# The opening of a triangle-and-pair kernel: weights turned ahead of x, evacuated on ScalarE, and the output weights prepared twelve steps later

## Chip, cores and metric

The kernel runs on one core of a Trainium2 chip. The metric is the device time of one execution in microseconds (us); the time before is the median of 3 runs, 3340.28 us (3338.49 to 3342.46).

## What is computed

x has the shape 1 x 384 x 384 x 128. Layer 0 is a triangle multiplication; layer 1 is a gated pair layer on its result. All in float32.

```python
z_n = layernorm(z, norm_g, norm_b)
a = linear(z_n, Wa, ba) * sigmoid(linear(z_n, Wga, bga))
b = linear(z_n, Wb, bb) * sigmoid(linear(z_n, Wgb, bgb))
x = einsum('bijd,bjkd->bikd', a, b)
x = layernorm(x, normo_g, normo_b)
z = z + linear(x, Wo, bo) * sigmoid(linear(z_n, Wgo, bgo))        # layer 0
left, right = z @ W_left + b_left + (z @ W_eq + b_eq), z @ W_right + b_right
out = left * right.sum(axis=2, keepdims=True) * sigmoid(z @ W_gate + b_gate)
y = layernorm(out @ W_out + b_out + z, ln_scale, ln_bias)          # layer 1
```

The change touches only the first projections (Wa, Wga, Wb, Wgb, Wgo with their biases) and the preparation of Wo and of layer 1's constants.

## The kernel before

The work has three stages: the projections of x (to about 1.4 ms), one 384 x 384 x 384 product per channel, and the output of layer 0 with all of layer 1. The order of every engine's instructions is the order of the Python text: there is no scheduler, each engine has its own queue and works it off in order, and a tile's buffer is given out again when its last reader is done. The change lies in the first stage.

x is read in tiles of 16 columns (fetch, fetch_parts), 128 rows each; the first tile comes in four parts of four columns. A step (step(s)) treats four columns, so a tile has four steps and the stage 288. For each four columns VectorE takes the statistics (L141, L142), POOL makes the factors rstd and off (norm_factors, L148 to L151), ScalarE normalises (normalise, zn, L160), TensorE turns the result (turn, ptr, L180) and ScalarE copies it out of PSUM (turned_out, zT, L191). Step s then projects zT on ga, a, gb and b (L246: pga, pa, pgb, pb) and on go (gate_project, pgo, L211). ScalarE does the sigmoids sga and sgb (L251) and gt (L198); VectorE combines pa with sga into at (L263), pb with sgb into bt (L276), and adds gate_bias to pgo (gs, L213). Step s also turns step s+1's columns. All projections share six PSUM buffers (pool p1p, tag pk), the turned x has two (tag ptr). From step 12 (CATCH_UP) on, POOL also adds b_out to each next tile of x and stores it as Z (residual, L171, L172), in the second step of a tile; before that four tiles are done at fixed steps.

The normalisation's gain and shift are folded into the weights: prepare(k) (L297) turns a weight on TensorE, copies it to SBUF as raw (L302), scales it by norm_g into wT (L304), multiplies raw by norm_b on TensorE (L306 for go, L309) and adds that to the bias (L310, or L307 for gate_bias, which is the row r_bgo broadcast to all partitions). The weights are loaded through ACT's queue (L339), everything else through SP's. Before the first step the text alternates quarters of x with weights: quarter 0; prepare ga, a; turn and evacuate quarter 0; quarter 1; prepare gb, b; quarter 2; nb_w (a broadcast of norm_b, L375); prepare go; quarter 3 (L364 to L377).

last_weights (L313 to L333) prepares Wo and layer 1's constants in three pieces, one after each of the steps 12, 13 and 14 (L381). The first piece is the copy of ob_w (L315), center, the turn of Wo (pt_o, which takes one of the six PSUM buffers) and two evacuations (raw_o, scaled_o); the third multiplies them (both_o, L327, L328).

## Time and profile before

| | |
|---|---|
| median of 3 runs | 3340.28 us |
| the profiled execution's own time | 3343.24 us |
| its span, first to last instruction | 3341.5 us |
| TensorE busy | 3293.7 us, 99% of the span |
| VectorE, ScalarE, POOL busy | 2666.1, 2311.3, 2091.9 us |
| mean granted TensorE clock | 0.994 |
| step 0's first projection (pga) starts | 15.00 us |
| one step in the steady part of the stage | 4.77 us |

The profile is one execution. Times in the views count from the first instruction of the span. A row of the timeline gives start, length, engine, line, operation, what is written from what, and, in brackets, how long the engine had been idle and what ended the wait. The engines are PE (TensorE), PEld (its weight loads, which overlap PE), DVE (VectorE), ACT (ScalarE), POOL and SP; a q behind a name is the queue that issues. The chain of work follows back, from the end, what released each piece. The clock column of the windows shows no throttle in the first 19 us even where the matmuls' lengths do, since its record begins later.

### The profile page before, as it was taken

How to read it: one execution, taken by the hardware profiler on the slowest of the kernel's cores; microseconds unless marked ns; L12 is line 12 of the kernel's file. 1: busy time of each engine (PE TensorE's matmuls, PEld its weight loads, DVE VectorE, ACT ScalarE, POOL GpSimd, SP SyncE). 2: the span in 40 equal slices, each digit the busy share in tenths (PEclk: the TensorE clock that was granted, in tenths of full speed). 3: DMA queues.
4: the chain of work that ended last, by engine and by line, in shares of the span. 5: the costliest groups of instructions: out<-in, count | busy, mean ns of one | idle time of the engine just before them, and what ended most of it. 6: DMA issues, size and time to landing. Idle time of an engine off the chain costs nothing.

```text
span 3341.5 us, 53397 instructions
## 1 busy us (share of the span) xinstructions
PE 3293.7 (99%) x15581; PEld 2191.3 (66%) x15581; DVE 2666.1 (80%) x8599; ACT 2311.3 (69%) x5488; POOL 2091.9 (63%) x1574
## 2 busy tenths in 40 slices
PE   8999999999999999999999999999999999999997
PEld 5555555555555555555555555588888888888885
DVE  8877777777777777455555555799999999999998
ACT  7778787877777788522222222378888888888887
POOL 7555555555555555355555555358888888888887
PEclk9999999999999999999999999999999999999998
DMA  6889899889888889899999999767777777777774
GB/s 226 265 256 273 278 282 282 278 279 281 280 269 264 268 275 282 254 337 318 312 315 311 312 311 304 258 231 262 261 263 262 262 262 264 264 263 263 263 265 142
DMA packets 675522, 910.52 MB, mean 272 GB/s; under 512 B 319520, under 2 KB 616480, under 8 KB 647712
## 3 DMA queue, kind: packets, MB, share of 16 engines
q1 hardware_dynamic: 634192, 680.28, 63.9%
q0 software_dynamic: 40320, 226.51, 19.3%
q8 instruction: 126, 2.06, 0.2%
q14 instruction: 164, 1.34, 0.1%
q10 hardware_dynamic: 720, 0.33, 0.0%
HBM read 454.04 MB, written 452.98 MB: 271 GB/s over the span
## 4 chain that ended last, share of the span: by engine, by line
PE 96%; DVE 2%; POOL 1%; DMA 1%; ACT 0%; issue 0%; POOLq 0%; ACTq 0%; SPq 0%; DVEq 0%
PE pm L488 22%; PE pga L246 8%; PE pa L246 7%; PE pgb L246 7%; PE pb L246 7%; PE py L602 7%; PE pf L592 7%; PE pgo L211 7%; PE pleft L643 7%; PE pg L645 7%; PE ptr L180 4%; PE ptr L566 4%; DMA G<-gt 0%; DVE py L608 0%; PE pg L656 0%
## 5 line engine op out<-in xcount | busy, mean ns | idle before, releaser
L488 PE MATMUL pm<-ab 128*128 128x384 f32 x2304 | 746.6, 487 | 5.8 <-DVE gs L213 5.8
L488 PEld LDWEIGHTS pm<-ab 128*128 128x128 f32 x2304 | 438.9, 191 | 312.4 <-DVE gs L213 6.7
L507 POOL TENSOR_TENSOR acc<-acc,xd 128x384 f32<-128x384 f32 x381 | 380.1, 998 | 362.4 <-DVE xd L500 362.2
L505 ACT ACTIVATE sq<-xd 128x384 f32<-128x384 f32 x381 | 188.5, 495 | 542.3 <-DVE xd L500 542.2
L276 DVE SCALAR_TENSOR_TENSOR bt<-pb,c_L_conv_bb,sgb 128x512 f32<-128x512 f32 x288 | 320.9, 1114 | 243.3 <-ACT zT L191 218.6
L160 ACT ACTIVATE zn<-xt,off,rstd 128x128 f32<-128x128 f32 x1152 | 503.3, 489 | 2.9 <-POOL off L151 2.8
L635 ACT ACTIVATE res<-res,off,rs 128x128 f32<-128x128 f32 x1152 | 482.5, 486 | 18.4 <-POOL off L629 15.7
L500 DVE TENSOR_TENSOR xd<-pm,acc 128x384 f32<-128x384 f32 x381 | 212.2, 557 | 343.3 <-POOL acc L507 321.3
L608 DVE SCALAR_TENSOR_TENSOR py<-py,acc,gr 128x128 f32<-128x128 f32 x1152 | 433.7, 377 | 2.2 <-PE py L602 1.6
L267 POOL DMA_DIRECT2D A<-at x72 | 85.4, 1186 | 539.2 <-DVE at L263 539.2
L251 ACT ACTIVATE sga<-pga,c_L_conv_bga 128x512 f32<-128x512 f32 x288 | 197.9, 687 | 267.6 <-PE pga L246 267.6
L211 PEld LDWEIGHTS pgo<-wT_go,zT 128*128 128x128 f32 x2176 | 285.7, 192 | 130.0 <-issue 66.5
L613 DVE BATCH_NORM_STATS2 st<-res 128x6 f32<-128x128 f32 x1152 | 361.4, 315 | 0.3
L675 POOL TENSOR_TENSOR res<-res,r_L_conv_ln_bias 128x1536 f32<-128x1536 f32 x94 | 324.6, 3453 | 7.4
L171 POOL TENSOR_TENSOR acc<-xt,r_L_conv_b_out 128x2048 f32<-128x2048 f32 x72 | 327.4, 4548 | 1.8
L592 PE MATMUL pf<-w_o,h 128*128 128x128 f32 x2304 | 321.2, 276 | 6.1 <-ACT w_o L574 5.3
L674 POOL TENSOR_TENSOR res<-res,r_L_conv_ln_scale 128x1536 f32<-128x1536 f32 x94 | 325.3, 3461 | 0.2 <-issue 0.2
L650 ACT ACTIVATE sg<-pg,c_L_conv_b_gate 128x384 f32<-128x384 f32 x384 | 223.0, 581 | 144.5 <-PE pg L645 92.6
L602 PE MATMUL py<-w_o,xr 128*128 128x128 f32 x2304 | 321.1, 276 | 0.0
L643 PE MATMUL pleft<-pairT,m_L_conv_W_left 128*128 128x384 f32 x768 | 313.1, 489 | 2.8 <-ACT pairT L568 2.8
L645 PE MATMUL pg<-pairT,m_L_conv_W_gate 128*128 128x384 f32 x768 | 311.1, 487 | 0.0
L141 DVE BATCH_NORM_STATS2 st<-xt 128x6 f32<-128x128 f32 x1152 | 305.5, 265 | 3.7 <-DMA xt<-in_x_dram 3.6
(142 smaller groups left out, 6826.8 us busy)
## 6 DMA issues: line engine op xcount, KB each, us to landing
A<-at POOLq DMA_DIRECT2D x72, 1024.0 KB, 8.5
Z<-acc POOLq DMA_DIRECT2D x72, 1024.0 KB, 8.2
G<-gt POOLq DMA_DIRECT2D x72, 1024.0 KB, 9.2
xr<-X SPq DMA_DIRECT2D x96, 768.0 KB, 6.0
gr<-G SPq DMA_DIRECT2D x96, 768.0 KB, 7.6
zr<-Z SPq DMA_DIRECT2D x96, 768.0 KB, 8.8
X<-xd SPq DMA_DIRECT2D x381, 192.0 KB, 6.2
xt<-in_x_dram SPq DMA_DIRECT2D x71, 1024.0 KB, 17.9
```

The lines of the kernel that those rows point to most:

```text
L160: nc.scalar.activation(g["zn"][:, c, :], g["x"][:, c, :], AF.Identity, bias=g["off"][:, c : c + 1], scale=g["rstd"][:, c : c + 1],)
L211: nc.tensor.matmul(pgo[:, c, :], lhsT=zT[:, c, :], rhs=wT["go"], start=True, stop=True)
L246: nc.tensor.matmul(pk, lhsT=wT[k], rhs=zT, start=True, stop=True)
L488: nc.tensor.matmul(products[d, ib], lhsT=ab[:, 0, q, ib * P : (ib + 1) * P], rhs=ab[:, 1, q, :], start=(q == 0), stop=(q == NB - 1),)
L507: nc.gpsimd.tensor_tensor(s1[:, ib, :], s1[:, ib, :], xd, ALU.add)
L592: nc.tensor.matmul(pf[:, q, :], lhsT=h[:, q * P : (q + 1) * P], rhs=w_o, start=True, stop=True)
L602: nc.tensor.matmul(py[:, q, :], lhsT=g["x"][:, i, q * P : (q + 1) * P], rhs=w_o0, start=True, stop=True)
L608: nc.vector.scalar_tensor_tensor(py[:, q, :], py[:, q, :], rs0[:, q, u : u + 1], g["g"][:, i, q, :], ALU.mult, ALU.mult)
L613: nc.vector.bn_stats(b["st"][:, k, q, :], b["res"][:, k, q, :])
L635: nc.scalar.activation(g["res"][:, i, q, :], g["res"][:, i, q, :], AF.Identity, bias=g["off"][:, i, q : q + 1], scale=g["rs"][:, i, q : q ...
L643: nc.tensor.matmul(pleft, lhsT=w_left, rhs=pairT, start=True, stop=True)
L645: nc.tensor.matmul(pg[:, 0:N], lhsT=w_gate, rhs=pairT, start=True, stop=True)
```

## The change

The five weights' turns are put ahead of x on TensorE, behind ten turns of the identity; two more such turns stand between the bias matmuls and x's first quarter (keep_busy). The copies out of PSUM and the scalings of all five weights go from VectorE to ScalarE, and so do the four bias columns; gate_bias's addition stays on VectorE and comes after all four quarters' statistics. Quarter 1's statistics move ahead of the normalisation of quarter 0. The loads of gb, b and go go through POOL's queue. Two of the parts of x are issued earlier among SP's small loads. The raw copies have five buffers instead of two. last_weights begins after step 24.

```diff
-        def prepare(k):
+        def turn_weight(k):
             both = ppp.tile([P, CT, P], FP, tag="pk", name="w_" + k)
-            pt, pb = both[:, 0, :], both[:, 1, :]
-            nc.tensor.transpose(pt, wT[k], ident)
-            raw = wp.tile([P, P], FP, tag="raw", name="raw_" + k, bufs=2)
-            nc.vector.tensor_copy(raw, pt)
-            scaled = ctile([P, P], "wT_" + k)
-            nc.vector.tensor_scalar(scaled, raw, ng, None, ALU.mult)
-            if k == "go":
-                nc.tensor.matmul(pb, lhsT=nb_w, rhs=raw, start=True, stop=True)
-                nc.vector.tensor_tensor(gate_bias, pb, gate_bias, ALU.add)
-            else:
-                nc.tensor.matmul(pb[:, 0:1], lhsT=raw, rhs=nb, start=True, stop=True)
-                nc.vector.tensor_tensor(bcol[k], pb[:, 0:1], bcol[k], ALU.add)
-            wT[k] = scaled
+            nc.tensor.transpose(both[:, 0, :], wT[k], ident)
+            return both
+
+        def raw_weight(k):
+            raw = wp.tile([P, P], FP, tag="raw", name="raw_" + k, bufs=5)
+            nc.scalar.copy(raw, halves[k][:, 0, :])
+            return raw
+
+        def scale_weight(k):
+            wT[k] = ctile([P, P], "wT_" + k)
+            nc.scalar.activation(wT[k], raws[k], AF.Copy, scale=ng)
...
-        for k in ("ga", "a", "gb", "b", "go"):
+        for k in ("ga", "a"):
             weight(k, nc.scalar)
+        for k in ("gb", "b", "go"):
+            weight(k, nc.gpsimd)
         nc.scalar.activation(warm, mhalf, AF.Sigmoid)
         ng, nb = column(L0 + "norm_g"), column(L0 + "norm_b")
         for k in ("ga", "a", "gb", "b"):
+            if k in ("ga", "gb"):
+                next(x_parts)
             bcol[k] = column(L0 + "b" + k)
-            if k in ("a", "b"):
-                next(x_parts)
...
+        def keep_busy(times):
+
+            idle = ppt.tile([P, CT, P], FP, tag="ptr", name="idle")
+            for k in range(times):
+                nc.tensor.transpose(idle[:, k % CT, :], ident, ident)
+
+        halves, raws = {}, {}
+        gated_and_not = ("ga", "a", "gb", "b")
+        keep_busy(10)
         first_quarter(0)
+        nc.vector.tensor_copy(nb_w, nb.to_broadcast([P, P]))
+        for k in gated_and_not + ("go",):
+            halves[k] = turn_weight(k)
+        for k in gated_and_not:
+            raws[k] = raw_weight(k)
+            scale_weight(k)
+        for k in gated_and_not:
+            nc.tensor.matmul(halves[k][:, 1, 0:1], lhsT=raws[k], rhs=nb, start=True, stop=True)
+        first_quarter(1)
         normalise(0, 0)
-        prepare("ga")
-        prepare("a")
+        keep_busy(2)
         turn(0)
+        raws["go"] = raw_weight("go")
         turned_out(0)
-        first_quarter(1)
+        for k in gated_and_not:
+            nc.scalar.activation(bcol[k], halves[k][:, 1, 0:1], AF.Identity, bias=bcol[k])
+        scale_weight("go")
+        pb = halves["go"][:, 1, :]
+        nc.tensor.matmul(pb, lhsT=nb_w, rhs=raws["go"], start=True, stop=True)
         normalise(0, 1)
-        prepare("gb")
-        prepare("b")
         first_quarter(2)
-        nc.vector.tensor_copy(nb_w, nb.to_broadcast([P, P]))
-        prepare("go")
         first_quarter(3)
+        nc.vector.tensor_tensor(gate_bias, pb, gate_bias, ALU.add)
         later = last_weights()
         for s in range(NT * TS):
             step(s)
-            if s >= CATCH_UP:
+            if s >= 2 * CATCH_UP:
                 next(later, None)
```

More of the change, by code (lines that the diff above doesn't have):

```diff
@@ L318, in last_weights @@
             nc.tensor.transpose(pt, wT["o"], ident)
-            raw, scaled = (wp.tile([P, P], FP, tag="raw", name=k + "_o", bufs=2) for k in ("raw", "scaled"))
+            raw, scaled = (wp.tile([P, P], FP, tag="raw", name=k + "_o", bufs=5) for k in ("raw", "scaled"))
             nc.vector.tensor_copy(raw, pt)
```

## The prediction

> **What bounds the kernel now.** I read the page first, then the chain of work for the first 30 us, then the timeline of the opening and of the place where the output weights are prepared. The page's busy times, and under them the chain that ended last, by engine:

> ```profile
> PE 3293.7 (99%) x15581; PEld 2191.3 (66%) x15581; DVE 2666.1 (80%) x8599; ACT 2311.3 (69%) x5488; POOL 2091.9 (63%) x1574
> ...
> PE 96%; DVE 2%; POOL 1%; DMA 1%; ACT 0%; issue 0%; POOLq 0%; ACTq 0%; SPq 0%; DVEq 0%
> ```

> TensorE sets the time almost everywhere. An edit of the opening therefore gains what it moves the start of TensorE's unbroken work, once, and that shift is carried to the end. The chain of work in the opening (start, us, what):

> ```profile
> 7.94 1.63 PE ptr L180 x4
> 9.57 0.23 PE w_gb L300
> ...
> 13.84 0.11 DVE nb_w L375
> 13.95 0.21 DVE raw_go L302
> 14.20 0.80 PE w_go L306 x2
> 15.00 1.71 PE pga L246 x2
> 16.71 1.71 PE pa L246 x2
> 18.41 1.45 PE pgb L246 x2
> ...
> 26.81 0.86 PE pga L246 x2
> ```

> x is turned by 9.57 us, but pga of step 0 stands in TensorE's queue behind prepare() of gb, b and go, and go waits for VectorE, which has quarter 2's statistics first. So step 0 starts at 15.00, not near 10.3. Second, pga and pa take 1.71 us where step 2's pga takes 0.86: half clock. pgb's 1.45 us fits 1.18 us at half rate and 0.27 at full, so full speed came at about 19.6. From pga of step 2 (26.81) on, steps follow every 4.77 us.

> The timeline where last_weights begins (after step 12), and POOL's and VectorE's rows at step 24 (start, us, engine, line, operation):

> ```profile
> 79.76 4.53 POOL L171 TENSOR_TENSOR acc<-xt,r_L_conv_b_out 128x2048 f32<-128x2048 f32 x1
> 80.02 4.37 DVE L315 COPY ob_w<-c_L_conv_normo_b 128x128 f32<-128x128 f32 x1
> ...
> 85.13 1.10 PE L246 MATMUL pga<-zT,wT_ga 128*128 128x512 f32 x2 [1.02 <-DVE scaled_o L321]
> ...
> 91.29 1.12 PE L246 MATMUL pga<-zT,wT_ga 128*128 128x512 f32 x2 [0.71 <-ACT zT L191]
> ```
> ```profile
> 138.87 4.55 POOL L171 TENSOR_TENSOR acc<-xt,r_L_conv_b_out 128x2048 f32<-128x2048 f32 x1
> ```
> ```profile
> 139.38 0.68 DVE L213 TENSOR_TENSOR gs<-pgo,r_L_conv_bgo 128x512 f32<-128x512 f32 x1
> ```

> A 128x128 copy that takes 0.19 us at 13.76 (nb_w) takes 4.37 here: it ends when POOL's addition does. TensorE then waits for a PSUM buffer (scaled_o) and for zT. pga of step 12 starts at 74.47 and of step 17 at 101.08: 26.61 us for five steps, 23.83 at 4.77 each, so the preparation costs 2.8 us, of which some 0.5 is its own TensorE work (0.11 + 2 x 0.22).

> [...] But the records of 5.8 to 12.3 us, transposes and small matmuls with gaps, did not lift the clock. [...]

> **The change, part by part.**

> Weights' loads. ACT issues two DMAs instead of five, so its table load (1.28) and warm end near 3.2 instead of 5.65. POOL issues gb, b, go from 1.4 us; at 0.57 each (its Z stores) that ends at 3.1, before rstd is due (5.39): free. Landing estimate: [...] go at 5.3 (bounds 4.5 and 7).

> TensorE ahead of x. Ten transposes of the identity from 1.4 us; at half rate some 0.22 each (twice the 0.11 of a warm one), done at 3.85, just when w_ga lands (3.88). Then five transposes, the last at about 5.8, four bias matmuls at 0.5 each until 7.9, and two transposes: all before the first turned quarter can start (zn at 7.40 + 0.5). Hidden; if go lands at 7, 0.8 us show at pga, of which 0.3 survive at pa (below).

> ScalarE. Four pairs of a copy from PSUM [...] and a scaling [...], overlapping a little: 0.6 to 0.7 a pair, from 4.35 to 6.8 or 7.15. zn cannot start before 7.40, when POOL has its factors. Hidden by 0.2 to 0.6 us. VectorE loses ten evacuations (0.26 to 0.31) and four small additions, and so does the statistics of quarters 1 to 3 earlier.

> Start of step 0. zn 7.40, turn until 9.57, zT until 10.2 (all as before), the go bias matmul between; pga at 10.4, 4.6 us earlier.

> The wait that the diff doesn't show. In the built program pa of step 0 gets the PSUM buffer of w_go, whose last reader is now the addition of gate_bias on VectorE. It stands behind all four quarters' statistics (done about 10.7) and needs r_bgo's load. That took

> ```profile
> r_L_conv_bgo<-in_L_conv_bgo_dram SPq DMA_DIRECT2D x1, 64.0 KB, 7.1
> ```

> from 6.44, so it landed at 13.5, 3.9 us after x's last part (9.65). With fewer loads in front, SP should issue it near 5.6, and x's last part should land at about 8.3: r_bgo at 12.2 (bounds 10 and 13.7). Addition 0.3: pa at 12.6. Queued behind pa: everything on TensorE. Before, pa starts at 16.71, so 4.1 us remain of the 4.6. ScalarE meanwhile does four bias columns (0.2 each), go's scaling and zn of quarter 1 until 13.1, in time for the turn after pgb.

> Clock. At 12.6 I take TensorE as still at half rate[...]. pa and pgb then run as slowly as before; [...] the shift at step 2 is 3.1 to 4.8, I take 3.9[...]. ScalarE and VectorE follow: at_0 waits for x's second tile (landing about 15) and is free by 17, before its buffer is wanted.

> last_weights from step 24 (also the first step of its tile). POOL's addition starts at 138.87 and gs ends at 140.06, so ob_w waits 3.4 us instead of 4.3. scaled_o is then done at about 144.1, when pga of step 26 is due; the wait of 1.1 vanishes, but gs of step 25 is still late and holds gt, zT and pga of step 27. Worked on by before's durations, steps 24 to 27 take 15.96 us against 16.82: gain 0.9 (bounds 0 and 2.2, the whole stall). Its loads are long in, and its results are wanted only after the first stage.

> Sum: 3.9 + 0.9 = 4.8 us. The profiled execution took 3343.24 (span 3341.5 and 1.7 around it): 3338.4. On the median of 3340.28: 3335.5. The profile lies 3 us above the median; that is of the size that half-clock stretches at the stage changes cost. One of them, in the table of windows (us, busy PE, PEld, DVE, ACT, POOL, clock, DMA):

> ```profile
> 1402.00:1409.00 7.00, 6.27 (x11) 3.43 (x12) 1.36 (x3) 2.19 (x4) 3.13 (x4) 0.52 1.00 344
> ```

> It stays by chance from run to run, and is in the range.

> **Rivals.**
> - The identity work does lift the clock. For: 15 transposes in 4.4 us. Against: [...] the cold 5.8 to 12.3 us of before. Then pa and pgb take 0.86: pga of step 2 at 21.5 instead of 26.81, 5.3 us, and with 0.9 the time is 3334.1.
> - r_bgo governs fully: it lands at 13.5 as before, pa starts at 13.9, 2.8 us are gained, and the new place of last_weights gains nothing: 3337.5. For: broadcast loads take 4.0 us even when the queues are quiet (ln_scale) and up to 11.0 behind x (b_out).
> - r_bgo lands by 11 and the stall at step 24 is all slack: 5.5 + 2.2 = 7.7, 3332.6. Against: 7.1 us to land, and the 1.2 us overlap of POOL with the copy's place.
> - Slower: POOL's loads of gb, b, go come late behind x's packets. All five turns stand ahead of x's turn on TensorE, so pga is go's landing + 3.3 (transpose 0.45, matmuls and idle 1.0, turn 1.0, zT 0.6, hand-overs). It loses from a landing at 12.6 on, 9.5 us after issue, 1 us for 1 us; at 15 the time is 3342.7. For: POOL's 1 MB transfers take 8.2 to 9.2. Against: these are 64 KB, and the queues were only 44% busy in the first 5 us.

> **Numbers.** Forecast 3335.5, chance 0.50, own range 3333.8 to 3337.0; clock lifted 0.17; r_bgo as before 0.20; larger gain 0.08; slower 0.05. Range 3331.5 to 3339.2. 0.2% is 6.7 us, about what a measurement of this kernel can tell from no change: faster by more means under 3333.6 (all of the larger gain, a third of the lifted clock, a tenth of the forecast: 0.19), slower by more means over 3347 (0.03).

> **What would show it.** pga of step 0 at 10.4 and not 15.0; a gap on TensorE after it that ends with gate_bias's addition; pa at 1.71 or 0.86 us; zn of quarter 0 still at 7.4; step 2's pga near 22.9; no long ob_w at 80 us, one of about 3.5 near step 24. I am wrong if zn waits for the weights on ScalarE, if go lands after 7 us, or if the steps' 4.77 us change.

## The result and the profile after

The changed kernel takes 3333.2 us (median of 14 executions, 3330.7 to 3335.88), the kernel before on the same chip 3341.24 (14 executions, 3338.49 to 3343.41): a ratio of 0.9977 with an interval of 0.997 to 0.9984, that is 8.0 us less (5.3 to 10.0). The forecast was 4.8 us less.

The page of the changed kernel, with the lines that answer to those of before (busy times; the chain that ended last, by engine):

```profile
PE 3293.1 (99%) x15593; PEld 2192.2 (66%) x15593; DVE 2661.7 (80%) x8585; ACT 2316.1 (70%) x5502; POOL 2095.1 (63%) x1577
...
PE 94%; DVE 4%; POOL 1%; DMA 0%; ACT 0%; issue 0%; POOLq 0%; ACTq 0%; DVEq 0%
```

TensorE's busy time is the same to 0.6 us, its new idle turns included; what has shrunk is the time in which it waits. The chain of work in its opening (start, us, what):

```profile
2.77 4.37 DMA w_go<-in_L_conv_Wgo_dram
7.18 0.47 PE w_go L299
...
9.16 0.53 PE idle L368 x2
9.69 0.87 PE ptr L180 x4
10.57 0.60 ACT zT L191
11.21 2.08 PE pga L246 x2
13.29 1.71 PE pa L246 x2
15.00 1.28 PE pgb L246 x2
...
23.23 0.86 PE pga L246 x2
```

The chain now begins with a load: w_go lands at 7.14 us, and its turn stands ahead of everything of x in TensorE's queue. pga of step 0 starts at 11.21 instead of 15.00 and pa follows it without a gap. pga of step 2 starts at 23.23 instead of 26.81: 3.58 us. The load of r_bgo and the addition that was forecast to hold pa:

```profile
r_L_conv_bgo<-in_L_conv_bgo_dram SPq DMA_DIRECT2D x1, 64.0 KB, 4.0
```
```profile
11.56 0.28 DVE L396 TENSOR_TENSOR r_L_conv_bgo<-w_go,r_L_conv_bgo 128x128 f32<-128x128 f32 x1
```

It was issued at 5.67 and landed at 9.7, so the addition only waited for the statistics in front of it. The chain where last_weights begins now (step 24):

```profile
128.08 0.86 PE pga L246 x2
...
133.71 3.44 DVE ob_w L313
137.88 1.10 PE pga L246 x2
...
144.06 1.12 PE pga L246 x2
```

Three steps take 15.98 us. Five steps from 24 on take 25.77 against 26.61 around step 12 before: 0.84 us. At the end of the first stage (its last pb: 1380.78 before, 1376.37 after) 4.41 us are gained, 3.58 and 0.84. So by the end of stage 1 the forecast's 4.8 was nearly all there, and of the 8.0 between the medians 3.6 us came afterwards, where the diff has no line. (The two profiled executions lie 10.1 us apart by their spans, 3341.5 and 3331.4, so pieces read from this one pair can be larger than the usual gain.) The largest piece is one wait at the join, where stage 1 ends and stage 2 begins: the first products of stage 2 (pm) wait for gs, the addition that empties the last gates' PSUM buffers. TensorE's waits before, then after (us in total, times, longest):

```profile
PE pm L488 <- DVE gs L213: 5.8, 1, 5.8
```
```profile
PE pm L507 <- DVE gs L213: 2.1, 1, 2.1
```

### The profile page after: what moved, and what is told of

Read it like the earlier page. It is cut to its first block, busy times and chain, and to the rows that moved or that the text cites. A ratio compares the mean times of both kernels' runs of the same rounds, so it can differ in the third digit from the quotient of the medians.

```text
span 3331.4 us, 53420 instructions
## 1 busy us (share of the span) xinstructions
PE 3293.1 (99%) x15593; PEld 2192.2 (66%) x15593; DVE 2661.7 (80%) x8585; ACT 2316.1 (70%) x5502; POOL 2095.1 (63%) x1577
## 3 DMA queue, kind: packets, MB, share of 16 engines
q14 instruction: 164, 1.34, 0.1%
## 4 chain that ended last, share of the span: by engine, by line
PE 94%; DVE 4%; POOL 1%; DMA 0%; ACT 0%; issue 0%; POOLq 0%; ACTq 0%; DVEq 0%
PE pm L507 22%; PE pga L246 8%; PE pa L246 7%; PE pb L246 7%; PE pgb L246 7%; PE pgo L211 7%; PE py L621 7%; PE pf L611 7%; PE pleft L662 7%; PE pg L664 7%; PE ptr L180 4%; PE ptr L585 4%; DVE py L627 1%; DVE st L632 1%; DVE h L599 1%; DVE res L612 1%
## 5 line engine op out<-in xcount | busy, mean ns | idle before, releaser
L627 DVE SCALAR_TENSOR_TENSOR py<-py,acc,gr 128x128 f32<-128x128 f32 x1152 | 419.3, 364 | 1.8 <-PE py L621 1.2
L632 DVE BATCH_NORM_STATS2 st<-res 128x6 f32<-128x128 f32 x1152 | 347.3, 303 | 0.3
L171 POOL TENSOR_TENSOR acc<-xt,r_L_conv_b_out 128x2048 f32<-128x2048 f32 x72 | 327.5, 4549 | 1.8
```

Source lines behind the costliest of these rows:

```text
L627: nc.vector.scalar_tensor_tensor(py[:, q, :], py[:, q, :], rs0[:, q, u : u + 1], g["g"][:, i, q, :], ALU.mult, ALU.mult)
L632: nc.vector.bn_stats(b["st"][:, k, q, :], b["res"][:, k, q, :])
```

## What the experiments were to tell apart

My theory after the result: 4.4 us belong to the opening and to the moved weights, as forecast; the join of the stages, untouched by the diff, gains because the new opening puts three loads on POOL's queue, ahead of the later stores of G (the finished gates, gt, written to memory), and the place in that queue decides how soon these land (A). Rivals: it depends on when stage 1 ends (B), or on the run (C). A fourth (D) was formed on the way, from a run that came out on the wrong side (e8). All ratios are against the kernel before, run beside it.

### The parts one by one, the loads, the idle turns

```diff
# e1_late_only, on the kernel before
-            if s >= CATCH_UP:
+            if s >= 2 * CATCH_UP:
```

> The kernel before with one edit: the output weights are prepared from step 24 instead of step 12; the opening stays the old one. Both theories on the rest agree for stage 1: it gains the 0.84 us that the two traces show around steps 12 to 17 (26.61 us) and 24 to 29 (25.77 us), from the missing stall behind the weight preparation. Where they part is the join of stage 1 and stage 2, where TensorE waited 5.77 us for gs before the change and 2.10 after it. Theory A (the shorter wait comes from the new opening, whose extra loads on POOL's queue shift what later lies beside the load of G): the join waits about 5.8 us here, and the whole is 3339.5 to 3341, 0.8 us below the kernel before. Theory B (the wait comes from when stage 1 ends, or from the moved weights): it waits about 2 to 3 us and the whole is 4 to 5 us below the kernel before. Theory C (it differs from run to run): either, and the median gains 0.8 with more scatter.

Measured: 3339.92 us, ratio 0.9998 (0.9989 to 1.0006). 1.1 us less, but the interval includes no change; the profile shows the join waiting 4.3 us.

```diff
# e2_opening_only, on the changed kernel
-            if s >= 2 * CATCH_UP:
+            if s >= CATCH_UP:
```

> The changed kernel with one edit: the output weights are prepared from step 12 again; the opening is the new one. Stage 1: pga of step 2 starts at 23.2 us as in the changed kernel, and the 0.84 us of the moved weights are lost again. Theory A (the join's shorter wait belongs to the opening and its loads on POOL's queue): 3.58 plus 3.67 gives 7.2 us below the kernel before, 0.8 above the changed one. Theory B (it belongs to the moved weights or to the time at which stage 1 ends): 3.6 us below the kernel before, 4.5 above the changed one. Theory C (run to run): 3.6 to 7, with the wait at the join of either size in the profile.

Measured: 3333.81 us, ratio 0.9978 (0.9971 to 0.9986): 7.2 us less. So the join's gain goes with the opening, and the moved weights are worth about what was forecast. Against B: e1 ends stage 1 earlier too (by 1.8 us in its profile) and doesn't have the gain. That is less than the change's 4.4, so e8 below, which ends it as early as the changed kernel, is the better test.

```diff
# e3_act_queue, on the changed kernel
-        for k in ("ga", "a"):
+        for k in ("ga", "a", "gb", "b", "go"):
             weight(k, nc.scalar)
-        for k in ("gb", "b", "go"):
-            weight(k, nc.gpsimd)
```

> The changed kernel with one edit: all five weights are loaded through ScalarE's queue, none through POOL's. It tests two things. First, whether w_go's arrival at 7.14 us sets the opening: with three more issues on ScalarE ahead of its table load the evictions of the turned weights start later, at about 5.7 us instead of 4.42, but go arrives some 1.5 us earlier; pga of step 0 then starts at 10.9 to 11.5 us, against 11.21. If the late go was the only thing, it comes to 10.4. Second, the join of the two stages: theory A (loads on POOL's queue shift what later lies beside the load of G) expects the wait for gs back at about 5.8 us and the whole 3.5 us above the changed kernel; theories B and C expect it within 1 us of the changed kernel.

Measured: 3332.87 us, ratio 0.9977 (0.9968 to 0.9987), as fast as the changed kernel with none of the weights on POOL's queue. That speaks against A, though the wait at the join was 3.7 us in its profile, between the 2.1 of B and the 5.8 of A. w_go was turned at 7.22 us and pga of step 0 started at 11.26, so ScalarE's queue brought it no sooner.

```diff
# e4_no_idle_turns, on the changed kernel
-        keep_busy(10)
...
-        keep_busy(2)
```

> The changed kernel without the twelve idle turns of the identity on TensorE. In the changed kernel's profile the clock rose only at 15.7 us, in a stretch of 3.4 us in which x's first matmuls ran. Theory 1 (turns don't count as work for the clock): the clock rises at the same place, pga of step 0 starts at 11.2 us, and the whole is within 0.4 us of the changed kernel. Theory 2 (the idle turns carry the clock): the clock rises one stretch of 3.4 us later, half the work of it is lost, and the whole is 1.3 to 1.7 us above the changed kernel.

Measured: 3333.88 us, ratio 0.998 (0.9972 to 0.9988): no difference from the changed kernel that can be told. The chain in its opening:

```profile
6.81 0.47 PE w_go L299
...
10.41 2.01 PE pga L246 x2
12.43 0.86 PE pa L246 x2
```

In this profile, without the idle turns, pa runs at full clock already, where the changed kernel's took 1.71 us. The turns did not carry the clock. Two of them even lie on the path: pga starts 3.60 us behind w_go's turn here, 4.03 there.

### Is it the place in POOL's queue?

```diff
# e5_three_loads on the kernel before; e6_five_loads the same with range(5) on the changed kernel
             step(s)
+            if s == 40:
+                for k in range(3):
+                    nc.gpsimd.dma_start(out=ctile([P, P], f"spare_{k}"), in_=ins[L0 + "Wgb"])
```

> The kernel before with three loads added on POOL's queue at step 40, 64 KB each, into tiles that nothing reads: the same number that the new opening moves to that queue, without the new opening. It tests why the store of G before the join landed after 10.25 to 10.28 us in all three profiles with weights on POOL's queue (the changed kernel, and with the weights at step 12 or without the idle turns), and after 11.3 to 12.8 us in the three others. Theory A (three earlier transfers on POOL's queue are enough[...]): G lands after about 10.3 us, TensorE waits about 2.1 us for gs, and the whole is 2.5 to 4 us below the kernel before. Theory C (it differs from run to run): G's landing stays anywhere from 10.3 to 12.8, and the whole is within 0.7 us of the kernel before.

> The changed kernel with five such unread loads on POOL's queue at step 40, so that with its three weights eight transfers more than in the kernel before have gone through that queue[...]. Theory A[...]: G lands after 11.3 to 12.8 us again, TensorE waits 3.7 to 5.8 us for gs, and the whole is 2 to 4 us above the changed kernel. Theory C: within 0.7 us of the changed kernel.

Measured: e5 3340.72 us, ratio 0.9999 (0.9991 to 1.0007), wait 5.5 us; e6 3332.12 us, ratio 0.9975 (0.9965 to 0.9984), wait 3.1 us. Neither moved. Theory A has fallen.

### Real products instead of turns; w_go out of the way

```diff
# e7_real_idle, on the changed kernel
...
-                nc.tensor.transpose(idle[:, k % CT, :], ident, ident)
+                nc.tensor.matmul(idle[:, k % CT, :], lhsT=ident, rhs=ident, start=True, stop=True)
...
-        keep_busy(10)
+        keep_busy(6)
...
             halves[k] = turn_weight(k)
+            keep_busy({"a": 3, "b": 1}.get(k, 0))
...
-        keep_busy(2)
+        keep_busy(1)
```

> The changed kernel with its idle turns replaced by real products of the identity with itself: six at the start, three behind the turn of w_a, one behind that of w_b, one ahead of the turns of x. In the six profiles so far the clock rose only behind a stretch of 3.4 us with over 2.4 us of real products in it, and not behind one with 3.2 us of work of which 2.0 were real. Theory 1 (only real products count for the clock): it rises at 4 to 9 us instead of 12.2 to 15.7, step 0 then runs at the full rate, pga of step 2 starts at 20 to 21 us instead of 21.15 to 23.07, and the whole is 1.5 to 2.5 us below the changed kernel. Theory 2 (work on the identity never lifts it, or the stretch must be filled by large products): the clock rises where it did, pga of step 0 is at 10.4 to 11.3 us, and the whole is within 0.5 us of the changed kernel.

Measured: 3332.45 us, ratio 0.9976 (0.9967 to 0.9986), not told apart from the changed kernel. The time hides that the products raised the clock. Its table of windows (stretch, its length, TensorE's busy time and instructions, clock, DMA share, GB/s) shows the clock full before x's first products, and lost again at once:

```profile
1.00:4.40 3.40, 3.05 (x14) 1.00 0.54 145
4.40:7.80 3.40, 2.81 (x22) 1.00 0.93 274
7.80:11.20 3.40, 3.19 (x11) 0.51 0.81 192
11.20:14.60 3.40, 3.40 (x5) 0.50 1.00 399
```

The clock's record begins at full rate at 4.48 us, falls to a half at 7.89 and is full again from 14.72. (The 1.00 of the first row is only where the record has not begun.) One burst was not enough here; step 0 still ran at half clock (pga 2.07 us, pa 1.71), and the forecast gain of 1.5 to 2.5 us didn't come.

```diff
# e8_go_last, on the changed kernel
-        for k in gated_and_not + ("go",):
+        for k in gated_and_not:
             halves[k] = turn_weight(k)
...
         turn(0)
-        raws["go"] = raw_weight("go")
+        halves["go"] = turn_weight("go")
         turned_out(0)
...
+        raws["go"] = raw_weight("go")
         scale_weight("go")
# and the bias product and gate_bias's addition behind step(0)
```

> The changed kernel with w_go turned behind the turns of x's first quarter, its eviction and its bias product later still (behind step 0): nothing of it is ahead of x any more. In the profiles so far pga of step 0 came 4.03 us behind the turn of w_go (7.18 to 11.21, 6.49 to 10.52, 7.22 to 11.26), and that turn waited for the load. Theory 1 (w_go's arrival sets the opening): pga of step 0 starts at 10.2 to 10.5 us whenever w_go lands, 0.1 to 0.9 us earlier, and the whole is 0.3 to 0.9 us below the changed kernel. Theory 2 (x's normalisation or the evictions would be as late): pga at 10.9 to 11.3 and no difference.

Measured: 3337.31 us, ratio 0.9989 (0.9983 to 0.9996): 4 us slower than the changed kernel, where I had expected a small gain. (e6 and e7, run beside it, took 3332.12 and 3332.45.) The opening was not the reason (pga of step 0 at 10.93 us, now behind w_gb, which landed at 6.34). The join was:

```profile
1390.73 1.46 PE L509 MATMUL pm<-ab 128*128 128x384 f32 x4
1397.70 2.93 PE L509 MATMUL pm<-ab 128*128 128x384 f32 x4 [5.51 <-DVE gs L213]
```

Stage 2 began as early as in the changed kernel (1390.73 us, against 1391.09), and G had landed as early (10.3 us after its issue in both), so theory B has no ground here; TensorE waited for a later gs. An edit of the opening had changed which gs that is. That gave theory D: the order in which the opening's PSUM tiles come free.

### The banks

The six buffers of stage 1 lie in PSUM banks 2 to 7, and each new tile gets the one that was freed first. Another order of release in the opening is therefore carried through all 288 steps. Stage 2's first products take banks 0, 4 and 3, whatever they last held. The banks are read off the built programs; the traces don't name them:

| kernel | bank 4 last held the gate of step | bank 3 |
|---|---|---|
| before, e1, e5, e12 | 286 | 287 |
| after, e2, e3, e4, e6, e7 | 284 | 282 |
| e8 | 287 | 286 |
| e9 (before, four spare tiles) | 284 | 282 |
| e10 (after, one spare tile) | 282 | 287 |
| e11 | 282 | 283 |

The traces bear the table out: in all fourteen profiles TensorE, where it waited, went on within 0.1 us of the end of the gs that the table gives for that product's bank. In the first four rows it waited at the second product (bank 4), in e10 and e11 at the third (bank 3).

The gates of 283 to 286 are emptied in one burst once G's store has landed and gt has its buffer; 287 hangs on the next store. VectorE's rows there, before and then after:

```profile
1400.19 2.48 DVE L213 TENSOR_TENSOR gs<-pgo,r_L_conv_bgo 128x512 f32<-128x512 f32 x4 [8.19 <-ACT gt L198]
```
```profile
1393.31 2.48 DVE L213 TENSOR_TENSOR gs<-pgo,r_L_conv_bgo 128x512 f32<-128x512 f32 x4 [5.71 <-ACT gt L198]
```

Before, pm went on at 1402.73, behind the fourth of the burst (1400.19 + 2.48 = 1402.67). After, it went on at 1394.65, behind the second.

```diff
# e9_before_banks, on the kernel before
+        for k in range(4):
+            nc.tensor.transpose(ppp.tile([P, CT, P], FP, tag="pk", name=f"spare_{k}")[:, 0, :], ident, ident)
         first_quarter(0)
# e10_after_banks, on the changed kernel: the same with range(1) ahead of the loop of the last gates
```

> The kernel before with four turns of the identity into spare PSUM tiles ahead of everything, where TensorE waits for its first weight anyway; nobody reads them. They change one thing: which PSUM bank each later tile of stage 1 gets. Stage 2's first products go to banks 0, 4 and 3. In the kernel before these two last belong to the gates of steps 286 and 287, the last ones, in the changed kernel to those of 284 and 282; here to 284 and 282 again. Theory D (the opening decides the order of the banks for the whole of stage 1, and with it which gs the first products of stage 2 wait for): TensorE waits for the second gs behind G's landing instead of the fourth, 1.2 us less for the same landing, 2.9 to 4.6 us instead of 4.3 to 5.8, and it falls to half clock for one stretch of 3.4 us less in part of the executions: the whole is 1.2 to 2.9 us below the kernel before. Rival (the join depends on when G lands and not on the banks): within 0.6 us of the kernel before.

> The changed kernel with one spare PSUM tile between the last step and the sixteen gates behind it, filled by one turn of the identity that nobody reads (0.2 us). It moves the banks of the last gates by one: stage 2's first three products then go to banks that were last those of 282 and 287, instead of 284 and 282. Theory D: the third of them waits for the gate of step 287, which hangs on the second landing of G, so that TensorE waits about 4 us instead of 2.1; the whole is 2 to 4 us above the changed kernel. Rival: within 0.6 us of it.

Measured: e9 3338.27 us, ratio 0.9992 (0.9985 to 0.9998): 2.4 us less than before, just clear of no change, from four unread turns. They did not speed up stage 1: stage 2 begins at 1395.79 us, against 1395.50 before. e10 3336.68 us, ratio 0.9988 (0.9981 to 0.9994): 3.5 us more than the changed kernel's median. In e9 the wait is 4.6 us for a landing after 12.76, where the kernel before waited 5.77 for 12.75. In e10 it is 6.2 us, where I expected about 4: G landed late here, 12.8 us after its issue. e9, then e10:

```profile
PE pm L490 <- DVE gs L213: 4.6, 1, 4.6
```
```profile
PE pm L509 <- DVE gs L213: 6.2, 1, 6.2
```

In e10 pm goes on at 1399.13, behind the single gs of step 287:

```profile
1398.39 0.69 DVE L213 TENSOR_TENSOR gs<-pgo,r_L_conv_bgo 128x512 f32<-128x512 f32 x1 [0.90 <-ACT gt L198]
```

With L for G's landing after its issue, the waits of each order lie on one line: wait = L - 6.98 for 286 (12.75: 5.8; 11.32: 4.3; 12.49: 5.5), and L - 8.16 for 284 (10.27: 2.1; 11.82: 3.7; 11.31: 3.1; 12.76: 4.6). The order is worth 1.2 us, plus what the shorter wait saves in clock. Theory D stands, but it is not the whole of the wait: of the 3.67 us by which the wait shrank between the two profiles of the result, 1.18 are the order, and 2.48 are G's earlier landing (10.27 against 12.75 us).

### All of it together

```diff
# e11_filled, on the changed kernel: e8's order for w_go, real products as in e7, and
+        for k in range(3):
+            nc.tensor.transpose(ppp.tile([P, CT, P], FP, tag="pk", name=f"spare_{k}")[:, 0, :], ident, ident)
         keep_busy(6)
...
             halves[k] = turn_weight(k)
+            keep_busy({"a": 4, "b": 4}.get(k, 0))
...
         keep_busy(2)
         turn(0)
         halves["go"] = turn_weight("go")
+        keep_busy(2)
```

> A version that joins what the runs point to: the changed kernel with real products of the identity (six at the start, four behind the turn of w_a, four behind that of w_b, two ahead of and two behind x's first turns) so that the clock stays up once it has risen, w_go turned behind x's first quarter, and three spare PSUM tiles at the start, so that stage 2's first products go to the banks of the gates of 282 and 283. Expected if the three readings hold: the clock rises at 3.7 to 7.1 us and stays, pga of step 0 starts at 10.2 to 10.9 us and pga of step 2 at 19.2 to 20.2 instead of 21.2 to 23.1; TensorE waits under 1 us for gs at the join for a landing of G after 10.3 us; the whole is 3328 to 3330.5, 3 to 5 us below the changed kernel. If the clock falls back in the opening (as it did with fewer products), 3330 to 3331.5; if the banks don't matter, 3330.5 to 3331.5.

Measured: 3328.56 us (5 executions, 3326.75 to 3329.62), ratio 0.9963 (0.9951 to 0.9976): 12.1 us less than the kernel before, run beside it, and 4 us more of gain than the change. The chain and, after it, TensorE's wait at the join:

```profile
10.80 1.13 PE pga L246 x2
11.93 0.86 PE pa L246 x2
12.79 0.86 PE pgb L246 x2
...
20.82 0.86 PE pga L246 x2
```
```profile
PE pm L515 <- DVE gs L213: 1.8, 1, 1.8
```

The clock's record begins at full rate at 6.47 us and stays there to 2139.8, the join included. pga of step 2 is 2.4 us earlier than in the changed kernel. It is a little later than expected (20.82, not 19.2 to 20.2), since the four products behind w_a (eight rows in the trace) took 1.53 us, 0.19 a row where the two rows of w_go's product at 15.83 took 0.22 together, and held w_gb's turn to 6.78. At the join the wait is 1.8 us although G landed only after 11.86; the expected wait of under 1 us was for a landing after 10.3 and stays untested.

### Is the landing fixed?

> The kernel before, unchanged, for a second look at one thing: the store of G ahead of the join landed 12.75 us after its issue in its profile and after 10.25 to 12.9 us in the others, whatever the opening. If this varies from run to run, it may land anywhere from 10.2 to 12.9 us here; if it is fixed by the program, at 12.75 again. In either case the wait of the second product of stage 2 for the fourth gs is the landing less 6.98 us, as it was in this kernel and in the two others with its order of banks.

Measured: the kernel before again, one execution, 3340.96 us. G landed after 12.02 us instead of 12.75, and the wait was 5.04: L - 6.98 once more. So the landing varies with the run. That it was 11.3 to 12.8 us in the five profiles with the old opening and 10.25 to 12.9 in the nine with a new one (six of them under 11.4) may be chance or not. So a part of the change's gain at the join may come from earlier landings too; what sets them, I couldn't settle.

## Why the forecast held, and where it was short

The median of 3333.2 us lies within the whole range forecast and just below the 3333.8 to 3337.0 of the main forecast. The parts that it named came to nearly the sizes forecast, in the opening partly by luck; a part that it did not name made up the rest.

**The opening: 3.9 forecast, 3.58 in the one profile.** The step "pga at 10.4, 4.6 us earlier" failed. "Landing estimate: ... go at 5.3 (bounds 4.5 and 7)" was 1.8 us too early and outside its bounds: a 64 KB load through POOL took 4.1 to 4.5 us here (w_go's 4.37, from 2.77 to 7.14; 3.6 to 4.9 in the other profiles). The 5.3 was my estimate alone: before has no load of that size through POOL. Through ScalarE's queue (e3) the same three took 4.1, 4.0 and 3.3, so the queue alone does not explain it. The forecast's own condition ("if go lands after 7 us") came true, and its "0.8 us show at pga" fits: 10.4 and 0.8, measured 11.21. The rival "slower" put pga 3.3 us behind go's landing. It was 4.07 (7.14 to 11.21): the four bias products and two idle turns in between took 2.0 us, not the 1.0 allowed there. pga starts 4.03 us behind w_go's turn: 7.18 and 11.21; 6.49 and 10.52 (e2); 7.22 and 11.26 (e3).

**r_bgo.** "r_bgo at 12.2 (bounds 10 and 13.7)" was too late: I kept the 7.1 us of the old load, and it took 4.0 (3.3 to 6.2 in the other profiles with a new opening, and in none of them did pa wait for it). The wait "that the diff doesn't show" was not there. Its place was taken by the late pga: pa came at 13.29 instead of 12.6. Two errors of the forecast, r_bgo too late and go too early, offset each other in part here, so the nearness of 3.58 to 3.9 is partly luck. So is that of the rival "r_bgo lands by 11 and the stall at step 24 is all slack", whose 7.7 us is the number nearest to 8.0: it was right on r_bgo (9.7), but its 5.5 us for the opening and 2.2 for step 24 were 3.58 and 0.84.

**ScalarE and x.** zn of quarter 0 started at 7.77 instead of 7.40: ScalarE waited 0.87 us for w_gb, which had landed late too, and its last scaling ended at 7.86 instead of 7.15. It didn't count, since w_go was later. Its copies took 0.24 to 0.27 us and its scalings 0.40 to 0.43, 0.65 to 0.67 a pair, as I had estimated (0.6 to 0.7); zn, with one pointer operand more than a scaling, takes 0.49.

**The clock.** "At 12.6 I take TensorE as still at half rate" was an estimate and held in this profile: pa takes 1.71 us, and the record is full from 15.71. The estimate "the shift at step 2 is 3.1 to 4.8" is what the other runs show: the clock came at 12.2 (e4) to 15.7 us with the new opening (e7 and e11, with their real products, aside), 17.4 to 19.8 with the old (19.5 in the kernel before). pga of step 2 starts at 26.6 us on the mean of five profiles with the old opening and at 22.2 on that of the four whose opening is the changed kernel's to the line (after, e2, e6, e10): 4.35 us, by the starts of its own rows, which lie some 0.2 us ahead of the chain's. The rival "the identity work does lift the clock" failed for turns (pa at 0.86 us without them in e4, at 1.71 with them in the changed kernel) and holds for products (full clock from 4.48 to 7.89 us in e7).

**last_weights.** 0.9 forecast, 0.84 measured, with ob_w at 3.44 us (forecast 3.4), ending again with POOL's addition (137.14 and 137.05; 84.39 and 84.29 before), and 15.98 us from step 24 to step 27 (15.96). Of the wait for scaled_o, forecast to vanish, 0.2 us are left.

**What was missing.** The forecast let every shift run to the end unchanged ("that shift is carried to the end"). It isn't: the opening also decided the order of the PSUM banks for 1.4 ms. e9 puts that at 2.4 us with its share of clock (0.7 to 5.0 by its interval), and it can be read off a built program ahead of any run. Together: opening 4.35 (the mean shift of pga of step 2, from profiles), weights 0.84, banks 2.4: 7.6 of the measured 8.0. Each of the two medians' differences, 2.4 and 8.0, is known only to about 2 us, so the agreement is closer than the numbers allow, and it leaves room for a share of G's landing. "It stays by chance from run to run" was right for the landing of G and for the half-clock stretch behind it (6.83 us in one profile of the kernel before, 3.41 in the other), and wrong for the wait's order, which is fixed.

## What to carry to other kernels

Where buffers are given out in order of release, one tile more or another order of release at the start decides which buffer is the last to come free a thousand microseconds later; before trusting a small difference, look at the waits at every change of stage, in stages that the edit doesn't touch too. A forecast of an opening is as good as its latest load: take the landing times of the same size and queue from the trace, with what else is in flight, and put nothing behind the last load that doesn't need it. What brought up TensorE's clock here was real products, and enough of them to last until the real work started: with 18 (e11) the record is full from 6.47 us on and step 0's pga took 1.13 us; with 11 (e7) the clock was lost at 7.89 us and pga took 2.07; with turns alone pga took 2.08.

## What the runs showed of the hardware

**What loses it.** Not every pause did here: it went with how the pause lay in the stretches. Windows of 3.41 us at the join, after and then e3:

```profile
1391.28:1394.69 3.41, 1.31 (x5) 1.00 1.02 370
1394.69:1398.11 3.42, 3.42 (x6) 0.50 1.02 357
```
```profile
1391.04:1394.46 3.42, 1.40 (x5) 1.00 1.02 417
1394.46:1397.87 3.41, 1.77 (x6) 1.00 0.98 333
```

A wait of 2.1 us left 1.31 us of work in one stretch, and the next ran at half clock. A wait of 3.7 us, spread over two stretches with 1.40 and 1.77, cost no clock. At the joins of all fourteen profiles every stretch with up to 1.34 us of work was followed by half clock, and no stretch that ran at full clock with 1.40 or more was. (Coming from half clock is another matter: 2.34 us in e6 and 2.55 in the kernel before were not enough to leave it.) All the work there is products of full width. In e7's opening the stretch from 4.48 to 7.89 us lost the clock with 2.81 us of work; only 1.32 us of it were products of the identity, the rest turns and products with a single column (the biases). Which of them counted, one stretch can't show.
